# Two graph layers on one core: the back-transform of the convolution cut into small pieces and tied to places in VectorE's queue

## The chip, the cores and the metric

The kernel runs on one core of a Trainium2 chip. The core's engines work from queues of their own: TensorE (PE, with its weight loads shown as PEld), VectorE (DVE), ScalarE (ACT), GpSimd (POOL), and SyncE (SP), which here only starts DMAs. Each engine takes its instructions in the order in which they stand in its queue; semaphores tie the engines together. The time is the device time of one execution in microseconds, and the median of several executions counts.

## The reference, cut to what matters

64 graphs of 256 nodes with 256 features. Layer 0 normalizes the adjacency matrix and multiplies; layer 1 has a convolution of 17 taps along the nodes, a message step with a soft adjacency, and a GRU cell. Each layer ends in a residual and a layer norm. All in float32.

```python
# layer 0
deg = adjacency_matrix.sum(axis=-1)
norm_adj = d_inv_sqrt[:, :, None] * adjacency_matrix * d_inv_sqrt[:, None, :]
h = jnp.einsum('bnm,bmf->bnf', norm_adj + alpha_eff * eye, x)
x = _layernorm(x + jnp.einsum('bnf,pf->bnp', h, W) + b)
# layer 1
h = relu(_bn(_conv1d(xc, conv1_w, 0), ...))
h = _bn(_conv1d(h, conv2_w, 8), ...)              # 17 taps along the nodes
x_conv = transpose(relu(h + xc))
A = jnp.exp(-dist) * mask                          # dist from three columns s of each node
x_nmp = jnp.einsum('bnm,bmd->bnd', A, relu(x @ w_msg.T + b_msg))
gi = concatenate([x_conv, x_nmp]) @ w_ih.T + b_ih
gh = x @ w_hh.T + b_hh
r, z = sigmoid(gi_r + gh_r), sigmoid(gi_z + gh_z)
x = _layernorm(x + (1 - z) * tanh(gi_n + r * gh_n) + z * x)
```

## The kernel before

The 64 graphs go in four groups (NQ = 4) of 16 (Q = 16). The long convolution is done in the frequency domain: the 256 nodes of a graph are cut into 8 tiles of 32 (GT = 8), each transformed over 48 points (FL = 48), so that a group gives 128 rows of every frequency. A group passes through these stages:

1. `layer0` (line 325) and `layer1` (390) for each graph. They are generators: every `yield` ends a piece, and the caller decides what is traced between two pieces. `layer0` has 3 pieces, `layer1` 7. On VectorE `layer0` ends with two scalar_tensor_tensor on x1 (line 383) and a layer norm; `layer1` adds a bias to h, once for each half of the nodes (410), and to msg (431), and multiplies aT by the adjacency (468). The fourth piece of `layer1` makes the forward transform (p_dft, 442), and ACT copies it to V (447).
2. `products` (515): in 12 steps the 23 complex frequencies, and the real ones in step 0, are multiplied by the transformed taps, three real products for a complex one. ACT and DVE write the results to M. V and M are the same tile VM, [128, 48, 256], under two names; so V of the next group can't be written before M of this one has been read.
3. The transform back, in place in M, all on VectorE: `real_transform` and `complex_begin` alongside the products, and `complex_end` (680) after them, made of `four` (560), `four_turned` (645), `turned` (588) and `output` (666). Each `output` writes a pair of points over all tiles to DRAM (xc_d) by a DMA in SP's queue. `complex_end` ends 18 pieces, of four to eight VectorE instructions each.
4. The gates, `gru` (753), for each graph, in 4 pieces: seven products for the first two gates by a scheme that saves an eighth (p_rz, 767), n (p_n, 804), the mixing with x1 and the layer norm. Before it come `load_conv`, `load_gate`, `residual` (a DMA of POOL's queue that adds x1 to the convolution's result), `transposed` and `input_sums` (POOL). All of it needs the convolution's result xc_d of the whole group.

Since V and M share a tile, the next group's first graphs are transformed into a tile of their own, V2, while this group is still being transformed back: AHEAD = 6 of 16 graphs. After `complex_end`, four ACT copies (984) bring V2 into V, and the other ten graphs follow with V as their goal, with four gate graphs (EARLY) in between, two pieces to a graph. The other 12 gate graphs, `late`, lie beside the next group's products, transform back and graphs ahead.

What is traced where is set at lines 949 to 991. In group 0 there are no gates yet: during the steps pieces of `begin` (the next group's graphs ahead) are taken, 2 to 4 per step, and then `merge(begin, end, 3)` traces one piece of `end` after every third of `begin`. In groups 1 and 2, 14 pieces of `late` go with the steps, then come 20 more with 6 of `begin` and 5 of `end`, then the graphs ahead with two pieces of `end` and two or three of `late` at each. In group 3, 14 of `late` go with the steps, and the rest is merged with `end`, two to one; then come all 16 gate graphs of group 3.

The order of tracing isn't that of the queues. A scheduler in the compiler makes the order of each engine's queue beforehand: by its own model of times it takes, among the instructions whose inputs it holds to be ready, the one traced first. So an instruction traced later goes ahead of an earlier one that is not ready yet. The queues are fixed after that; on the chip an instruction that waits holds up all behind it on its engine. Tiles come from pools with a fixed number of buffers: four PSUM banks for the layers (`bank`) and four for products and gates (`accbank`).

Of the kernel before, what the change touches and what calls it, by code (L numbers as in the profile page):

```python
# [14 lines left out]
P = 128  # L15
# [11 lines left out]
def kernel(  # L27
# [55 lines left out]
    def accbank(name):  # L83
        return psacc.tile([P, 512], F32, tag="acc", name=name)

# [239 lines left out]
    def layer0(g):  # L325
# [56 lines left out]
        for c in range(NCH):  # L382
            nc.vector.scalar_tensor_tensor(
                x1[:, c, :], p[:, c, :], dis[:, c : c + 1], x_t[:, c, :], op0=ALU.mult, op1=ALU.add
            )
# [4 lines left out]
    def layer1(g, V, place):  # L390
# [13 lines left out]
        for c in range(NCH):  # L404
            p = bank("p_conv1")[:, : D + NSE]
            for k in range(DCH):
                nc.tensor.matmul(  # L407
                    p, x1T[:, k, c * P : (c + 1) * P], wc1[:, k, :], start=k == 0, stop=k == DCH - 1
                )
            nc.vector.tensor_tensor(h[:, c, :], p, bc1, op=ALU.add)  # L410
# [20 lines left out]
        nc.vector.tensor_tensor(msg, p, bmsg_t.unsqueeze(1).to_broadcast([P, NCH, D]), op=ALU.add)  # L431
# [36 lines left out]
        nc.vector.tensor_mul(aT, aT, adjT[:, :, 0:3:2, :])  # L468
# [91 lines left out]
    def four(re, im):  # L560


        by = im - re
        sub2(blocks(re, by, 2), blocks(re + 2, by, 2))
        sub2(blocks(re, by), blocks(re + 1, by))
        add2(M[:, re + 2, :], M[:, im + 3, :])
        sub2(M[:, im + 2, :], M[:, re + 3, :])
# [31 lines left out]
    def real_transform():  # L599
# [13 lines left out]
        four(8, 12)  # L613
# [31 lines left out]
    def four_turned(re, im, angle):  # L645
# [4 lines left out]
        c2, t2 = turned(re + 2, im + 2, 2 * angle)  # L650
        stt(z[2], t2, -c2, z[0], op0=ALU.mult, op1=ALU.add)
        stt(z[0], t2, c2, z[0], op0=ALU.mult, op1=ALU.add)
        yield
        c1, t1 = turned(re + 1, im + 1, angle)
        c3, t3 = turned(re + 3, im + 3, 3 * angle)
        stt(z[3], t3, -c3 / c1, t1, op0=ALU.mult, op1=ALU.add)
        stt(t1, t3, c3 / c1, t1, op0=ALU.mult, op1=ALU.add)
        stt(z[1], t1, -c1, z[0], op0=ALU.mult, op1=ALU.add)
# [5 lines left out]
        yield  # L664

    def output(q, n, re, im):
# [5 lines left out]
        by = [real_part(t[:, j, :], x, y, 2 * math.pi * (n + 16 * j) / FL) for j in range(2)]  # L672
        low = min(re, im)
# [4 lines left out]
        )  # L678

    def complex_end(q):  # L680

        four(CR, CI)
        yield
        for outs in (((0, 0, 0), (8, 1, 0)), ((4, 2, 0), (12, 3, 1))):
            for n, i, exchanged in outs:
                output(q, n, (CR, CI)[exchanged] + i, (CI, CR)[exchanged] + i)
            yield

        add2(M[:, CR + 4 : CR + 6, :], M[:, CI + 6 : CI + 8, :])
        sub2(M[:, CI + 4 : CI + 6, :], M[:, CR + 6 : CR + 8, :])  # L690
        yield
        for n, re, im, angle in ((2, CR + 4, CI + 4, math.pi / 4), (6, CI + 6, CR + 6, 3 * math.pi / 4)):
            low = min(re, im)
            c, t = turned(re + 1, im + 1, angle)
            stt(blocks(low + 1, 16), t, -c, blocks(low, 16), op0=ALU.mult, op1=ALU.add)
            stt(blocks(low, 16), t, c, blocks(low, 16), op0=ALU.mult, op1=ALU.add)
            yield
            output(q, n, re, im)
            output(q, n + 8, re + 1, im + 1)
            yield  # L700
        for n, re, im, angle in ((1, CR + 8, CI + 8, math.pi / 8), (3, CI + 12, CR + 12, 3 * math.pi / 8)):
            yield from four_turned(re, im, angle)
            output(q, n, re, im)
            output(q, n + 8, re + 1, im + 1)
            yield
            output(q, n + 4, re + 2, im + 2)
            output(q, n + 12, im + 3, re + 3)
            yield
# [44 lines left out]
    def gru(g):  # L753
# [26 lines left out]
        nc.vector.tensor_add(first, half(p15), brz_t)  # L780
# [6 lines left out]
        nc.vector.tensor_add(trz[:, 1:3], trz[:, 1:4:2], half(p34))  # L787
# [7 lines left out]
        for c in range(NCH):  # L795
# [13 lines left out]
            nc.vector.tensor_add(gn, p.rearrange("p (i d) -> p i d", i=2), bn_t)  # L809
# [17 lines left out]
            nc.vector.scalar_tensor_tensor(y, t, 3.0, y, op0=ALU.add, op1=ALU.mult)  # L827
# [31 lines left out]
    def run(stage):  # L859
        for _ in stage:  # L860
            pass

# [59 lines left out]
    gate = ctx.enter_context(tc.tile_pool(name="gate", bufs=2))  # L922
    ahead = ctx.enter_context(tc.tile_pool(name="ahead", bufs=1))


    AHEAD = 6
    V2 = ahead.tile([P, FL, DCH, AHEAD * GT], F32, name="V2")
    EARLY = 4
# [19 lines left out]

    late = nothing()
    for q in range(NQ):  # L950
# [3 lines left out]
        if more:  # L954
            if q:
                others = [both(take(late, 3 if i % 3 == 0 else 2), take(end, 2)) for i in range(AHEAD)]
# [5 lines left out]
        for step in range(STEPS):  # L962
# [5 lines left out]
            if q:  # L968
                run(take(late, (0, 1, 1, 1, 1, 1, 2, 1, 2, 1, 2, 1)[step]))
            else:  # L970
                run(take(begin, 2 + step // 4))
        run(real)
        if not q:
            run(merge(begin, end, 3))
        elif more:
            run(merge(merge(take(late, 20), take(begin, 6), 3), take(end, 5), 5))
            run(begin)
        else:
            run(merge(late, end, 2))
        if more:  # L980
            run(late)
            run(end)
            for f in range(0, FL, 12):
                nc.scalar.copy(V[:, f : f + 12, :, : AHEAD * GT], V2[:, f : f + 12])
            early = gates(q, range(EARLY))
            others = [take(early, 2) for _ in range(Q)]
            run(graphs(first, range(AHEAD, Q), V, others))
            run(early)
            late = gates(q, range(EARLY, Q))
# [55 lines left out]
```

## Time and profile before

| | us |
|---|---|
| runs | 2195.01, 2198.28, 2193.91; median 2195.01 |
| the profiled execution's own time | 2197.18 |
| its span, first to last instruction | 2195.4 |
| mean granted TensorE clock over the span | 0.981 |

The page gives each engine's busy time and its share of the span. Its second part cuts the span into 40 slices of some 55 us; a digit is the busy share in tenths. A stretch of the trace can be asked for by its bounds: the answer has the busy time of each engine in it, the number of instructions in brackets, the granted TensorE clock, and the share and rate of the DMA engines. Matmuls overlap one another, so the time from one to the next is less than the 380 ns that a record of one shows.

The four groups' products begin on PE about 298, 690, 1190 and 1690 us into the span. After about 1960 us only gates of group 3 are left. These rows are the costliest of VectorE's on the tile VM over the whole span (line, operation, count; busy us, mean ns):

| line | what | x | us, ns |
|---|---|---|---|
| 546, 547 | subtract, and 2x - y, of `sub2` | 104 each | 72.6, 698; 72.4, 696 |
| 675 | the two points of `output` | 128 | 55.3, 452 |
| 575, 577 | `real_part` | 100, 72 | 45.4, 465; 30.4, 427 |
| 583, 585 | `imaginary_part` | 24, 20 | 14.5, 605; 9.9, 495 |

In all VectorE is busy 491.65 us with instructions on VM, of 1554.1.

### The profile page before, as it was taken

What the parts mean: (1) busy time and instruction counts of PE and PEld (TensorE: products, weight loads), DVE (VectorE), ACT (ScalarE), POOL (GpSimd) and SP (SyncE); (2) the same over time, 40 slices, a digit from 0 to 9 for tenths busy, and PEclk for the clock granted to TensorE, in tenths of its full rate; (3) what the DMA queues carried; (4) which work ended last, traced back from release to release, by engine and by line L of the source; (5) the groups of instructions that cost most, each with busy time, mean ns of one, the idle gap of its engine ahead of it and who ended that gap; (6) DMA issues with size and microseconds to landing.
All of it is one profiled execution on the core that took longest, in us unless ns stands there. A gap on an engine that the chain in (4) does not pass through costs nothing.

```text
span 2195.4 us, 28939 instructions
## 1 busy us (share of the span) xinstructions
PE 2070.3 (94%) x9805; PEld 1754.5 (80%) x9805; DVE 1554.1 (71%) x3743; ACT 828.8 (38%) x1838; POOL 664.1 (30%) x641
## 2 busy tenths in 40 slices
PE   5999989969999997999999998899999999899998
PEld 4878768758888886888888887788888887678887
DVE  5555548875568799655556889855555879977666
ACT  2656533445441122456552222446553112222222
POOL 2444310113321234223222224322231223344442
PEclk8999989979999999999999999999999999999999
DMA  3766657443337644333335654433333654444441
GB/s 98 222 194 201 218 159 223 154 134 115 99 112 220 201 120 125 115 101 107 108 113 174 204 163 121 130 106 113 103 95 117 207 163 116 119 120 111 104 113 54
DMA packets 251823, 305.83 MB, mean 139 GB/s; under 512 B 18797, under 2 KB 230337, under 8 KB 251674
## 3 DMA queue, kind: packets, MB, share of 16 engines
q1 hardware_dynamic: 183338, 199.93, 30.0%
q10 hardware_dynamic: 45280, 68.04, 8.8%
q0 software_dynamic: 23056, 36.01, 8.3%
q8 instruction: 78, 1.28, 0.2%
q14 instruction: 71, 0.57, 0.1%
HBM read 200.79 MB, written 103.12 MB: 138 GB/s over the span
## 4 chain that ended last, share of the span: by engine, by line
PE 50%; DVE 14%; issue 6%; POOL 6%; ACT 4%; DMA 0%; ACTq 0%; POOLq 0%; SPq 0%; DVEq 0%
PE p_rz L767 18%; PE p_n L804 9%; PE p_k L497 8%; PE p_nmp L473 2%; PE p_out L379 2%; PE p_dft L442 2%; PE p_conv L407 2%; PE p_hT L369 2%; POOL sums L749 1%; POOL ln_rs L304 1%; PE p_msg L428 1%; PE p_dist L466 1%; POOL sums L751 1%; POOL sums L750 1%; DVE gn L809 1%
## 5 line engine op out<-in xcount | busy, mean ns | idle before, releaser
L767 PE MATMUL p_rz<-wrz,sums 128*128 128x256 f32 x1536 | 357.4, 384 | 19.4 <-DVE gn L809 9.8
L804 PE MATMUL p_n<-wn,inputs 128*128 128x256 f32 x1536 | 351.2, 381 | 16.1 <-DVE first L780 15.5
L767 PEld LDWEIGHTS p_rz<-wrz,sums 128*128 128x128 f32 x1536 | 289.8, 191 | 70.9 <-issue 15.8
L804 PEld LDWEIGHTS p_n<-wn,inputs 128*128 128x128 f32 x1536 | 285.8, 190 | 61.8 <-DVE first L780 18.5
L767 PE MATMUL p_rz<-wrz,inputs 128*128 128x256 f32 x1152 | 272.6, 380 | 1.5 <-ACT inputs L739 1.5
L304 POOL TENSOR_TENSOR ln_rs<-ln_rs,neg_half 128x2 f32<-128x2 f32 x129 | 100.3, 777 | 538.9 <-DVE ln_rs L303 453.1
L767 PEld LDWEIGHTS p_rz<-wrz,inputs 128*128 128x128 f32 x1152 | 216.9, 190 | 32.6 <-ACT inputs L739 3.5
L340 POOL TENSOR_TENSOR dis<-deg,neg_half 128x2 f32<-128x2 f32 x64 | 48.5, 758 | 428.8 <-DVE deg L338 322.7
L816 ACT ACTIVATE nn<-gn 128x256 f32<-128x256 f32 x128 | 53.2, 416 | 324.9 <-DVE gn L813 324.5
L497 PE MATMUL p_k<-u,VM 128*128 128x256 f32 x736 | 175.1, 380 | 0.0
L314 ACT ACTIVATE x_g<-x_g,ln_mr,ln_rs 128x256 f32<-128x256 f32 x128 | 70.0, 593 | 256.4 <-DVE ln_mr L312 256.4
L497 PEld LDWEIGHTS p_k<-u,VM 128*128 128x128 f32 x736 | 138.6, 190 | 19.6 <-DMA u<-ud 0.8
L407 PE MATMUL p_conv<-wc,xn 128*128 128x259 f32 x512 | 130.4, 398 | 14.4 <-ACT xn L399 13.8
L442 PE MATMUL p_dft<-fwd,h 128*128 128x240 f32 x512 | 119.8, 378 | 24.3 <-ACT h L411 23.4
L748 POOL TENSOR_TENSOR sums<-inputs 128x384 f32<-128x384 f32 x64 | 69.5, 1086 | 230.4 <-issue 172.2
L369 PE MATMUL p_hT<-adjT,x 128*128 128x256 f32 x512 | 125.9, 391 | 8.3 <-DVE adjT L352 8.1
L442 PEld LDWEIGHTS p_dft<-fwd,h 128*128 128x128 f32 x512 | 97.1, 194 | 40.9 <-ACT h L411 32.9
L473 PE MATMUL p_nmp<-aT,msg 128*128 128x256 f32 x512 | 123.8, 385 | 2.6 <-DVE aT L468 2.6
L407 PEld LDWEIGHTS p_conv<-wc,xn 128*128 128x128 f32 x512 | 98.6, 196 | 34.5 <-ACT xn L399 18.8
L379 PE MATMUL p_out<-w,hT 128*128 128x256 f32 x512 | 124.2, 386 | 0.9 <-ACT hT L374 0.7
L362 POOL TENSOR_TENSOR x_t<-x_t,b_t 128x512 f32<-128x512 f32 x64 | 84.6, 1323 | 128.5 <-ACT x L361 88.3
L428 PE MATMUL p_msg<-wmsg,xn 128*128 128x256 f32 x512 | 122.8, 383 | 0.0
(153 smaller groups left out, 3852.5 us busy)
## 6 DMA issues: line engine op xcount, KB each, us to landing
u<-ud SPq DMA_DIRECT2D x284, 256.0 KB
xn_d<-xn ACTq DMA_DIRECT2D x64, 512.0 KB
inputs<-xn_d SPq DMA_DIRECT2D x64, 512.0 KB
ud<-u_set POOLq DMA_DIRECT2D x39, 480.0 KB, 6.2
adj_t<-in_adj_dram SPq DMA_DIRECT2D x64, 256.0 KB
x_t<-in_x_dram SPq DMA_DIRECT2D x64, 256.0 KB
x_d<-x ACTq DMA_DIRECT2D x64, 256.0 KB
x_g<-x_d SPq DMA_DIRECT2D x64, 256.0 KB
```

The source lines that it names most:

```text
L304: nc.gpsimd.tensor_tensor(rs[:, : len(chunks)], rs[:, : len(chunks)], neg_half[:, : len(chunks)], op=ALU.pow)
L314: nc.scalar.activation(y[:, c, :], y[:, c, :], AF.Identity, bias=mr[:, c : c + 1], scale=rs[:, c : c + 1])
L362: nc.gpsimd.tensor_tensor(x_t, x_t, b0_t.unsqueeze(1).to_broadcast([P, NCH, D]), op=ALU.add)
L369: nc.tensor.matmul(p[:, k, :], x1[:, mc, k * P : (k + 1) * P], adjT[:, mc, 1 - mc : 3 - mc, :].rearrange("p n q -> p (n q)"), start=mc == ...
L379: nc.tensor.matmul(p[:, c, :], hT[:, k, c * P : (c + 1) * P], w0[:, k, :], start=k == 0, stop=k == DCH - 1)
L407: nc.tensor.matmul(p, x1T[:, k, c * P : (c + 1) * P], wc1[:, k, :], start=k == 0, stop=k == DCH - 1)
L428: nc.tensor.matmul(p[:, c, :], x1T[:, k, c * P : (c + 1) * P], wmsg[:, k, :], start=k == 0, stop=k == DCH - 1)
L442: nc.tensor.matmul(p[:, t0 * FL : t1 * FL], h[:, c, k * P : (k + 1) * P], fwd[:, first : first + t1 - t0, :].rearrange("p t f -> p (t f)") ...
L473: nc.tensor.matmul(p[:, k, :], msg[:, mc, k * P : (k + 1) * P], aT[:, mc].rearrange("p n q -> p (n q)"), start=mc == 0, stop=mc == NCH - 1,)
L497: nc.tensor.matmul(p[:, j * D : (j + 1) * D], v[:, k, :], u[:, k, :], start=k == 0, stop=k == DCH - 1)
L767: nc.tensor.matmul(p[:, j * D : (j + 1) * D], a[:, k], wrz[:, b, k], start=k == 0, stop=k == HALF - 1)
L804: nc.tensor.matmul(p[:, o * D : (o + 1) * D], lhsT, w, start=j == 0, stop=j == len(part) - 1)
```

## The change

Four things are changed.

- The pieces of the transform back become small: `four`, `four_turned`, `output` and `complex_end` yield after every two VectorE instructions. `real_transform` still runs its `four` at once.
- Six places in `layer0` and `layer1` and five in `gru` are marked (`mark`): the x1 operations, both h, msg and aT; `first`, the sum trz[:, 1:3], both gn, and y. A new function `paced` runs a main stage and, after each of its pieces, adds a rate for each instruction that was marked in it; for every whole unit it traces one piece of the transform back under `tc.issue_after(i)`. That gives each instruction which the piece traces on VectorE an edge to the marked one, so that the scheduler can't put it ahead of it in VectorE's queue. It is an edge of order alone, with no semaphore. Other engines' instructions, the output DMAs among them, get none.
- In group 0, 12 graphs are made ahead in place of 6, into a V2 of twice the size. For room, the pool `gate` is opened only once this V2 is closed, after the copies to V; four graphs remain to be made beside the four early gate graphs, with five pieces of `early` at each in place of two. From group 1 on V2 has 6 graphs as before.
- What is traced beside what: `end` no longer goes with the graphs ahead by `both`, nor by `merge`, but by `paced` with the rates 1.2, 0.85, 0.85 and 1.15 pieces for each mark in the four groups. In group 0 each step takes 3 pieces of `begin`. In group 3 a step takes `step % 2` pieces of `late`, 6 in all.

```diff
+    def paced(main, other, rate):
+
+        marks.clear()
+        due = 0
+        for _ in main:
+            for i in marks:
+                due += rate
+                while due >= 1:
+                    due -= 1
+                    with tc.issue_after(i):
+                        next(other, "end")
+            marks.clear()
+            yield
...
-            nc.vector.tensor_tensor(h[:, c, :], p, bc1, op=ALU.add)
+            mark(nc.vector.tensor_tensor(h[:, c, :], p, bc1, op=ALU.add))
...
-        nc.vector.tensor_add(first, half(p15), brz_t)
+        mark(nc.vector.tensor_add(first, half(p15), brz_t))
...
         sub2(blocks(re, by, 2), blocks(re + 2, by, 2))
+        yield
         sub2(blocks(re, by), blocks(re + 1, by))
+        yield
         add2(M[:, re + 2, :], M[:, im + 3, :])
+        yield
         sub2(M[:, im + 2, :], M[:, re + 3, :])
...
         by = [real_part(t[:, j, :], x, y, 2 * math.pi * (n + 16 * j) / FL) for j in range(2)]
+        yield
         low = min(re, im)
...
-    gate = ctx.enter_context(tc.tile_pool(name="gate", bufs=2))
-    ahead = ctx.enter_context(tc.tile_pool(name="ahead", bufs=1))
-
-
-    AHEAD = 6
-    V2 = ahead.tile([P, FL, DCH, AHEAD * GT], F32, name="V2")
     EARLY = 4
+
+    def open_ahead(graphs):
+
+        scope = ExitStack()
+        pool = scope.enter_context(tc.tile_pool(name="ahead", bufs=1))
+        return scope, graphs, pool.tile([P, FL, DCH, graphs * GT], F32, name="V2")
...
+    RATES = (1.2, 0.85, 0.85, 1.15)
+
+
+    scope, AHEAD, V2 = open_ahead(12)
     late = nothing()
     for q in range(NQ):
...
-                others = [both(take(late, 3 if i % 3 == 0 else 2), take(end, 2)) for i in range(AHEAD)]
+                others = [take(late, 3 if i % 3 == 0 else 2) for i in range(AHEAD)]
...
-                run(take(late, (0, 1, 1, 1, 1, 1, 2, 1, 2, 1, 2, 1)[step]))
+                run(take(late, (0, 1, 1, 1, 1, 1, 2, 1, 2, 1, 2, 1)[step] if more else step % 2))
             else:
-                run(take(begin, 2 + step // 4))
+                run(take(begin, 3))
         run(real)
         if not q:
-            run(merge(begin, end, 3))
+            run(paced(begin, end, RATES[q]))
         elif more:
-            run(merge(merge(take(late, 20), take(begin, 6), 3), take(end, 5), 5))
-            run(begin)
+            run(paced(chain(merge(take(late, 20), take(begin, 6), 3), begin), end, RATES[q]))
         else:
-            run(merge(late, end, 2))
+            run(paced(late, end, RATES[q]))
+            run(end)
         if more:
             run(late)
             run(end)
             for f in range(0, FL, 12):
                 nc.scalar.copy(V[:, f : f + 12, :, : AHEAD * GT], V2[:, f : f + 12])
+            if q == 0:
+                scope.close()
+                gate = ctx.enter_context(tc.tile_pool(name="gate", bufs=2))
             early = gates(q, range(EARLY))
-            others = [take(early, 2) for _ in range(Q)]
+            others = [take(early, 5 if q == 0 else 2) for _ in range(Q)]
             run(graphs(first, range(AHEAD, Q), V, others))
             run(early)
+            if q == 0:
+                scope, AHEAD, V2 = open_ahead(6)
+                ctx.enter_context(scope)
             late = gates(q, range(EARLY, Q))
```

## The prediction

> **What bounds the kernel now.** I read the page's busy shares and its 40 slices first, then the windows around the dips, the waits of PE there, the timeline inside the deepest dip, and the chain of waits last.
>
> ```profile
> PE 2070.3 (94%) x9805; PEld 1754.5 (80%) x9805; DVE 1554.1 (71%) x3743; ACT 828.8 (38%) x1838; POOL 664.1 (30%) x641
> ...
> PE   5999989969999997999999998899999999899998
> ...
> DVE  5555548875568799655556889855555879977666
> ...
> PEclk8999989979999999999999999999999999999999
> ```
>
> PE is busy 94%, but its slices dip four times (slices 9, 16, 25, 35), each time where DVE shows 8 or 9. Each dip follows the products of one group of 16 graphs, where DVE transforms back. The windows on those stretches (length, PE busy, PE weight loads, DVE, ACT, POOL, granted clock, DMA share, GB/s):
>
> ```profile
> 414.00:478.00 64.00, 43.85 (x202) 34.13 (x200) 61.88 (x177) 26.25 (x61) 8.54 (x8) 0.90 0.40 128
> 478.00:500.00 22.00, 20.39 (x79) 15.96 (x80) 9.47 (x31) 14.84 (x31) 10.81 (x11) 0.75 0.64 155
> 780.00:920.00 140.00, 125.51 (x576) 105.20 (x575) 127.04 (x302) 46.88 (x103) 52.54 (x46) 0.96 0.46 129
> 1290.00:1410.00 120.00, 105.22 (x478) 88.51 (x477) 117.55 (x269) 33.76 (x73) 43.48 (x38) 0.96 0.44 123
> 1800.00:1960.00 160.00, 141.85 (x649) 118.41 (x648) 150.48 (x307) 35.59 (x72) 62.24 (x55) 1.00 0.41 114
> ```
>
> The same windows for VectorE's instructions on the transform's tile VM alone:
>
> ```profile
> 414.00:478.00 64.00, 46.41 (x111) 0.90 0.40 128
> ...
> 1290.00:1410.00 120.00, 56.40 (x113) 0.96 0.44 123
> 1800.00:1960.00 160.00, 67.34 (x124) 1.00 0.41 114
> ```
>
> And the stretch ahead of the last dip, where group 3's products run:
>
> ```profile
> 1690.00:1800.00 110.00, 110.00 (x517) 96.67 (x516) 87.98 (x170) 20.29 (x40) 21.45 (x19) 1.00 0.69 208
> ```
>
> I price lost PE time as stretch minus matmuls times full-rate pitch. That pitch is 110/517 = 0.213 us in the last line, 188.20/916 = 0.2055 in the layer-rich stretch from 500 to 690, about 0.2105 for mixtures. Lost: 414 to 500: 86 - 281 x 0.2055 = 28 us. 780 to 920: 140 - 576 x 0.2105 = 19. 1290 to 1410: 120 - 478 x 0.2105 = 19. 1800 to 1960: 160 - 649 x 0.211 = 23. Together 89 us of 131 lost in all (2195.4 - 9805 x 0.2105); most of the rest is setup and tail, which the change leaves alone.
>
> Why PE loses is plainest in the first dip (timeline: start, duration, instruction, idle time before it in brackets):
>
> ```profile
> 461.54 17.36 SPq L676 DMA_DIRECT2D xc_d<-VM  x8
> ...
> 468.33 0.43 DVE L410 TENSOR_TENSOR h<-p_conv,bc 128x259 f32<-128x259 f32 x1
> ...
> 469.73 0.63 ACT L411 ACTIVATE h<-h 128x512 f32<-128x512 f32 x1 [9.30 <-DVE h L410]
> ...
> 470.41 3.56 PE L442 MATMUL p_dft<-fwd,h 128*128 128x240 f32 x8 [9.56 <-ACT h L411]
> ```
>
> From 458.7 to 468.3 DVE does transform operations back to back (L662, L577, L675 and so on); the h addition, whose matmuls were done at 458.7, waits behind them, then ACT, then PE for 9.56 us. The scheduler held the transform operations to be ready sooner. In the three later dips no single wait is so long: DVE is 90 to 98% full and PE loses 0.5 to 3.9 us at a time, for `first` (L780), gn (L809) and xn.
>
> **What the Trainium skill says.** "TensorE: Matmul & The Clock Gate", section "What's actually happening", says that an idle window of about 3.4 us throttles the PE clock until a busy window releases it. The trace agrees: after the 9.56 us wait the clock is 0.75 (second window), while the last dip, made of short waits, stays at 1.00. So closing long gaps pays twice. "Perfetto Trace Analysis", section "Optimization Strategy", says that where the contended engine changes over time, interleaving the regimes may help; the trace has such regimes: DVE 97% in the first dip, 61% (115.95 of 190) from 500 to 690. "SBUF — State Buffer", section "SBUF: two separate sides", says that DVE operations with two SBUF inputs and GpSimd lock each other out of a shared port; the trace's 256-element transform operations take 386, 416 and 1215 ns (least, median, most), in line with it. So a transform operation costs more among gates, where POOL is busier: 46.41/111 = 0.42 us beside layers, 56.40/113 = 0.50 and 67.34/124 = 0.54 beside gates. No page prices an order edge.
>
> **The change, part by part.** *The back-transform's work* is the same: 116 DVE instructions per group (32 pairs for 16 outputs, 8 in `four`, 44 others) and 16 output DMAs on SP. Cut at the new yields it has 4 + 8 + 2 + 12 + 32 = 58 pieces of two instructions, 0.84 us each beside layers, 1.0 to 1.1 beside gates.
>
> *The edge* adds no wait: a piece only stands behind the marked operation on DVE's queue. It forbids the block seen at 458 to 468. Behind each mark one or two pieces (0.8 to 2 us) may delay what follows on DVE: trz behind `first`, L810 behind gn, the second h; PE waits for the first two through banks. I cost this at nothing where DVE has idle time, since the next operation of a chain is usually not ready at once; it is the bad rival below. POOL, ACT and SP get no edge; SP's output DMAs follow data, one at a time instead of eight together (17.36 us), so the loads behind them go earlier.
>
> *Group 0.* The steps take 3 pieces of `begin` each, 36 as before (2 to 4). Of 12 graphs ahead, 9 remain: 90 main pieces, 9 x 6 = 54 marks; at 1.2 all 58 pieces are out by mark 48.3, graph 8 of 9. A layer graph costs PE 13.2 us (about 64 matmuls x 0.2055) and DVE 7.4 (rows of section 5 and of the groups by line, 7.2; from 500 to 690 115.95 less 4.6 gate graphs at 10.5, over 9.1 layer graphs, 7.4). Pieces add 7.2 x 0.84 = 6.0: DVE 13.4 against PE 13.2. So it is just saturated for 8 graphs: 2 us short, and 6 for waits at a full queue (estimate: PE's small waits in the later dips are 1 to 2 us per 15). Left 8 to 9 of 28: gain 19. Against it: V2 is twice as large, so the four ACT copies (12 x 1159 ns for three groups) take about 9.3 us rather than 4.6, and the gate pool opens only after them. Graph 12's PE work and two layer0 cover this, not wholly: 2 us back. Net 17. Then 4 graphs instead of 10 stand beside 4 gate graphs; each graph's 13.2 us hides the first loads. The remaining five `early` pieces per graph sum to the same 20.
>
> *Groups 1 and 2.* The products are unchanged. Then 34 gate pieces (8.5 gate graphs at 5 marks) and 8 graphs of layer work give about 82 marks; at 0.85 the end is out by mark 68. A gate graph costs PE 70 x 0.211 = 14.8, DVE 8.7 packed ((219.73 - 126.28)/10.7 from 1690 to 1936) to 10.5 (1960 to 2100: 99.29 over 9.45). Pieces add 5 x 0.85 x 1.0 = 4.2: 12.9 to 14.7 against 14.8. Before, the first five gate graphs carried about 7 us of transform each. So DVE is full but no longer over. I leave 8 of 19 us: gain 11 each, 22. The end is out long before the V copies.
>
> *Group 3.* The steps now take 6 gate pieces rather than 14, so 42 (10.5 graphs, 53 marks) run under the end; at 1.15 its last piece stands behind mark 51. Per graph 8.7 + 5 x 1.15 x 1.09 = 15.0 on DVE against 14.8: saturated, not over. Steps: PE 60 (284 x 0.211) + 1.5 x 14.8 = 82; DVE 59 + 13 to 16, fits. Last transform operation at 1690 + 84 + 155 = 1929 (1934.4 now). Behind it the chain to group 3's first sums: xc write (2.9 us, 1934.47 to 1937.37), xc load (3.2 to the accumulating DMA at 1940.54), that DMA, about 3, transposes, ACT, POOL sums (0.6 + 0.9 + 1.1): about 13. The work left for PE then is about 4 us, so some 9 are bare, where before gates covered most. The sums' matmuls start at 1943 to 1949 instead of 1953.8. Gain 6.
>
> Sum 17 + 22 + 6 = 45: from the profiled execution's own 2197.2 us (span 2195.4) to 2152. The median of the runs, 2195.0, is 2.2 lower; forecast 2150.
>
> **The rivals.**
> A. As above: own range 2132 to 2170. Chance 0.48.
> B. Everything recovered: 79 of the 89 us, 2116. For it: total DVE work is below PE's in every group. Against: DVE full at the rates of groups 0 and 3. 0.10.
> C. Only the long block goes: group 0 gains 17, the gate stretches stay DVE-bound, since 10.5 + 4.2 already meets 14.8 and waits come on top: 2178, 2164 to 2197. 0.21.
> D. Slower: the pins sit at the gates' bank releases. `first` (L780) and gn (L809) are among five marks, and PE already waits 15.5 us in 12 waits for one and 9.8 in 9 for the other. If a piece of 0.84 us lands between each and the next release, each of the 27.5 gate graphs loses 1.7 us more and nothing of the gate stretches is won: +46 - 17 = +29, 2224. It decides from 17/27.5 = 0.6 us per gate graph beyond today's loss. For it: a full in-order DVE queue; against: fewer pieces per gate graph than now in groups 1 and 2. Group 3's bare chain, up to 13 us, adds to it. 0.21.
>
> **How the numbers follow.** About 0.2% (4.4 us) is what a measurement here tells from no change. Faster: A, B and most of C (0.16): 0.74. Same: 0.03 of C and 0.03 of D: 0.06. Slower: 0.02 of C, 0.18 of D: 0.20. The range from 2126 to 2206 holds A, C, about two fifths of D and a third of B; some 0.19 is outside.
>
> **What would show it.** Right: no DVE block of transform operations over 3 us beside layers; no PE wait over 4 us and a clock at 1.00 from 415 to 540; PE at 94% or more in the three later stretches; 12 x 1.16 us copies become 8 of 1.16 and 4 of 2.3. Wrong: waits for `first` and gn growing beyond 50 us in sum (D); DVE at 97% with PE below 90% in the gate stretches (C); a PE gap over 13 us ahead of group 3's gates, or PE starved in its steps.

## The result, and the profile after

The changed kernel takes 2190.7 us (median of four runs, 2189.66 to 2191.19) against 2195.4 for the kernel before beside it (four runs): 0.9976 of its time, interval 0.9959 to 0.9994. The forecast was 2150. The sign was right and the size was not: some 5 us came where 45 were forecast. The profiled execution has a span of 2188.8 us against 2195.4.

The page's busy shares and its slices after:

```profile
PE 2071.8 (95%) x9805; PEld 1753.1 (80%) x9805; DVE 1558.0 (71%) x3743; ACT 831.9 (38%) x1838; POOL 654.3 (30%) x641
...
PE   5999999988999998999999999899999999989998
...
DVE  5555558786568798865557889875556989967766
...
PEclk8999999999999999999999999999999999989999
```

The dip to 6 in slice 9 is gone from PE's row; the clock's dip that stood there is gone too, and another stands in slice 36. Shallow dips to 8 remain at slices 9 and 10, 16, 26 and 36. The same four stretches as before, the first 6 us earlier, the third 10 (columns as in the prediction):

```profile
408.00:494.00 86.00, 75.41 (x363) 59.16 (x362) 70.00 (x212) 48.71 (x114) 18.84 (x20) 1.00 0.38 124
780.00:920.00 140.00, 130.04 (x607) 109.54 (x606) 121.63 (x283) 51.05 (x111) 47.10 (x46) 0.98 0.42 120
1280.00:1400.00 120.00, 111.29 (x527) 95.45 (x526) 108.73 (x235) 38.62 (x84) 44.08 (x43) 0.99 0.43 119
1800.00:1960.00 160.00, 141.63 (x631) 119.87 (x630) 133.37 (x279) 35.21 (x73) 60.25 (x58) 0.94 0.42 114
```

Counted as the prediction counted them, the stretches lose 11 us (86 - 363 x 0.2055; 28 before), 12 (19), 9 (19) and 27 (23). A reader who stopped here would book 17 + 7 + 10 - 4 = 30 us of gain. The span is only 6.6 us shorter, and most of that comes from elsewhere. So the stretches must be completed to whole stages. A stage runs here from the start of a group's first matmul into p_real to the next group's. In the kernel before these starts are at 297.7, 652.4, 1171.8 and 1689.7 us; the 690 and 1190 given ahead of the prediction for the second and third group are too late. So the stretch from 500 to 690, which gave the pitch of 0.2055, holds 38 us of group 1's products; 500 to 652 alone has 739 matmuls in 152 us, 0.2057 for each, and the pitch stands. In the table, "ahead" is from the first p_dft (group 0's own graphs) to group 0's products, and the last stage runs to the end of the span:

| us | ahead | group 0 | group 1 | group 2 | group 3 | span |
|---|---|---|---|---|---|---|
| before | 248.1 | 354.6 | 519.5 | 517.9 | 505.7 | 2195.4 |
| after | 241.7 | 355.1 | 515.5 | 513.0 | 513.5 | 2188.8 |
| difference | -6.4 | +0.5 | -4.0 | -4.9 | +7.8 | -6.6 |
| forecast | 0 | -17 | -11 | -11 | -6 | |

Group 0 gives all its gain back inside its own stage, groups 1 and 2 keep 4 and 5 us of 7 and 10, group 3 loses, and 6 us come from a place that the prediction didn't look at.

**Ahead.** POOL around 275 us in the kernel before (timeline: start, duration, instruction, idle time before it in brackets):

```profile
274.57 0.99 POOL L748 TENSOR_TENSOR sums<-inputs 128x384 f32<-128x384 f32 x1 [11.11 <-DMA x_g<-x_d]
275.52 0.71 POOL L340 TENSOR_TENSOR dis<-deg,neg_half 128x2 f32<-128x2 f32 x1
276.19 0.71 POOL L304 TENSOR_TENSOR ln_rs<-ln_rs,neg_half 128x2 f32<-128x2 f32 x1
```

One of the sums for gate graph 0, which PE first reads at 410 us, had been put ahead of dis and ln_rs of the layers. It waits 11.11 us for its DMA, and the layers wait behind it: between 240 and 300 us PE waits 5.3 us for h at one place (wait, us in all, times, longest):

```profile
PE p_dft L442 <- ACT h L411: 5.3, 1, 5.3
```

After, the gate pool opens only after the copies to V, so nothing of the gates can stand there.

**Group 0's handover.** Three more windows after, and the timeline at the copies:

```profile
494.00:520.00 26.00, 23.86 (x115) 18.64 (x114) 20.63 (x65) 15.09 (x36) 5.52 (x5) 1.00 0.32 102
520.00:560.00 40.00, 32.28 (x150) 26.23 (x149) 14.25 (x51) 26.62 (x48) 12.55 (x14) 0.91 0.60 178
560.00:647.00 87.00, 84.75 (x403) 71.50 (x404) 53.17 (x113) 30.88 (x70) 31.95 (x31) 1.00 0.32 88
```

```profile
529.77 4.13 ACT L1016 COPY VM<-V 128x2304 f32<-128x2304 f32 x2
...
536.33 2.11 ACT L1016 COPY VM<-V 128x2304 f32<-128x2304 f32 x1 [0.50 <-ACT xn L485]
...
538.35 0.58 ACT L407 COPY xn<-p_x1T 128x512 f32<-128x512 f32 x1
538.98 3.82 PE L415 MATMUL p_conv<-wc,xn 128*128 128x259 f32 x8 [5.61 <-ACT xn L407]
```

From 520 to 560 PE does 150 matmuls: 40 - 150 x 0.2055 = 9 us are lost, at a clock of 0.91. ACT is in V2's four copies, of 2.1 us each, and what PE needs from ACT (xn) stands behind them: PE waits 5.61 us. Another 2 us go from 494 to 520 and 4 after 560. The kernel before at its own handover and behind it:

```profile
500.00:560.00 60.00, 59.83 (x297) 50.38 (x296) 33.29 (x91) 31.69 (x76) 16.44 (x18) 1.00 0.31 93
560.00:652.00 92.00, 90.37 (x444) 76.32 (x443) 54.81 (x140) 44.69 (x104) 28.93 (x29) 1.00 0.35 101
```

Over the whole stage the kernel before lost 2 + 28 - 1 + 1 = 30 us (554, 281, 297 and 444 matmuls in windows from 298, 414, 500 and 560 to 652), the changed one 3 (548 matmuls from 292 to 408) + 11 + 2 + 9 + 4, about 30 again.

**Group 1's handover.** The window and the timeline where its gate graphs end and the next layers begin, after:

```profile
836.00:862.00 26.00, 20.01 (x84) 16.35 (x83) 24.70 (x50) 7.80 (x18) 12.71 (x12) 0.87 0.54 150
862.00:960.00 98.00, 93.27 (x451) 77.24 (x450) 78.23 (x212) 45.55 (x103) 24.22 (x23) 1.00 0.35 113
```

```profile
835.68 1.03 PE L385 MATMUL p_out<-w,hT 128*128 128x256 f32 x4
...
839.86 2.24 DVE L596 SCALAR_TENSOR_TENSOR turn<-VM 128x256 f32<-128x256 f32 x1
...
844.18 0.86 DVE L390 SCALAR_TENSOR_TENSOR x<-p_out,dis,x_t 128x256 f32<-128x256 f32 x2
...
855.76 3.82 PE L415 MATMUL p_conv<-wc,xn 128*128 128x259 f32 x8 [3.17 <-ACT xn L407]
```

26 - 84 x 0.2105 = 8 us are lost in these 26: p_out is done at 836.7, but x1's addition starts at 844.18, behind a queue of transform pieces and gate work on DVE (24.70 busy of 26.00). PE has gate products to do until 852.6, with waits of 1.27 us for POOL's sums and 1.55 for `first`; then only the new graph's chain is left, and it waits 3.17 for xn. The clock in the window is 0.87. Another 5 us go from 862 to 960.

**Group 3's end.** After, at the last output:

```profile
1932.13 0.51 SPq L692 DMA_DIRECT2D xc_d<-VM  x1
...
1934.81 9.96 SPq L729 DMA_DIRECT2D xc_g<-xc_d  x3
...
1938.85 1.24 POOL L740 DMA_DIRECT2D xc_g<-x_d  x1 [12.14 <-DMA xc_g<-xc_d]
...
1943.27 1.11 PE L751 MATMUL p_xcT<-ident,xc_g 128*128 128x128 f32 x4 [9.97 <-DMA xc_g<-x_d]
...
1947.61 5.44 PE L781 MATMUL p_rz<-wrz,sums 128*128 128x256 f32 x18
```

The gates of group 2 are used up; PE waits 9.97 us for output, load and addition, before the transposes can start. Measured from the start of its own products the last output is at 1932.1 - 1675.3 = 256.8 us, where it was at 244.7 before: it comes 12 us later, with nothing left beside it.

PE's waits over the whole span, after:

```profile
PE p_conv L415 <- ACT xn L407: 23.2, 18, 5.6
PE p_n L818 <- DVE first L794: 13.0, 11, 3.0
PE p_dft L450 <- ACT h L419: 12.2, 18, 2.4
PE p_xcT L751 <- DMA xc_g<-x_d: 10.8, 2, 10.0
```

### The profile page after: what moved, and what is told of

Same layout as the page of the kernel before. It is cut to its first block, busy times and chain, and to the rows that moved or that the text cites. A ratio compares the mean times of both kernels' runs of the same rounds, so it can differ in the third digit from the quotient of the medians.

```text
span 2188.8 us, 28989 instructions
## 1 busy us (share of the span) xinstructions
PE 2071.8 (95%) x9805; PEld 1753.1 (80%) x9805; DVE 1558.0 (71%) x3743; ACT 831.9 (38%) x1838; POOL 654.3 (30%) x641
## 4 chain that ended last, share of the span: by engine, by line
PE 42%; DVE 11%; issue 7%; POOL 5%; ACT 4%; DMA 1%; ACTq 0%; POOLq 0%; SPq 0%; DVEq 0%
PE p_rz L781 16%; PE p_n L818 8%; PE p_k L505 7%; PE p_nmp L481 2%; PE p_hT L375 2%; POOL ln_rs L310 1%; PE p_out L385 1%; PE p_dft L450 1%; POOL sums L764 1%; POOL sums L765 1%; POOL sums L763 1%; PE p_conv L415 1%; PE p_msg L436 1%; PE p_dist L474 1%; ACT inputs L753 1%
## 5 line engine op out<-in xcount | busy, mean ns | idle before, releaser
L781 PE MATMUL p_rz<-wrz,sums 128*128 128x256 f32 x1536 | 352.5, 382 | 5.1 <-POOL sums L764 2.6
```

The costliest lines, as they stand in the source:

```text
L781: nc.tensor.matmul(p[:, j * D : (j + 1) * D], a[:, k], wrz[:, b, k], start=k == 0, stop=k == HALF - 1)
```

## The experiments

Theory: the transform pieces cost what was forecast; the gain is given back at three handovers (V2's copies in group 0, gates to layers in 1 and 2, the end of group 3). Rivals: the edges themselves cost it; the pieces still cost PE as much as before; 12 graphs ahead are the wrong place. Each was timed beside the kernel before. Stages, in us, of one profiled execution each (the ratio is that of the times). That execution can lie off the median of its runs, by some 3 us at most in ten of the rows; e1's lies 4.3 below it, e11's 6.4 above:

| | ahead | g0 | g1 | g2 | g3 | span | median | ratio, interval |
|---|---|---|---|---|---|---|---|---|
| e1_gate_late | 240.3 | 360.5 | 519.6 | 518.2 | 505.7 | 2190.5 | 2196.6 | 0.9999, 0.999 to 1.0008 |
| e2_last_old | 240.0 | 355.8 | 515.4 | 512.9 | 505.8 | 2177.2 | 2181.3 | 0.9935, 0.9921 to 0.995 |
| e3_copies_dve | 240.2 | 348.6 | 515.8 | 512.7 | 514.0 | 2178.3 | 2183.2 | 0.9947, 0.9933 to 0.9961 |
| e4_no_edges | 240.2 | 356.5 | 519.7 | 518.6 | 507.5 | 2189.6 | 2193.2 | 0.9989, 0.9981 to 0.9996 |
| e5_both | 241.6 | 348.4 | 518.4 | 512.7 | 505.6 | 2177.3 | 2176.2 | 0.992, 0.9908 to 0.9933 |
| e6_no_back0 | 241.6 | 340.7 | 515.6 | 513.7 | 505.6 | 2167.9 | 2169.6 | 0.9887, 0.9874 to 0.9901 |
| e7_pace_last | 239.9 | 349.4 | 517.6 | 512.7 | 507.0 | 2173.0 | 2175.1 | 0.9919, 0.9906 to 0.9932 |
| e8_first_old | 240.1 | 365.3 | 514.3 | 512.7 | 505.7 | 2184.4 | 2187.0 | 0.9972, 0.9963 to 0.9981 |
| e9_two_rates | 239.7 | 349.3 | 512.7 | 510.2 | 505.6 | 2163.9 | 2166.3 | 0.9882, 0.9867 to 0.9897 |
| e10_no_back1 | 240.0 | 349.3 | 500.4 | 514.9 | 505.7 | 2157.5 | 2159.2 | 0.9849, 0.9835 to 0.9862 |
| e11_nine | 241.5 | 362.2 | 514.2 | 515.1 | 506.3 | 2189.7 | 2185.0 | 0.9969, 0.9957 to 0.998 |
| e12_three_tenths | 241.5 | 348.2 | 519.6 | 517.0 | 505.8 | 2183.2 | 2182.2 | 0.9941, 0.9927 to 0.9954 |

Group 1, with nothing changed in it, takes 514.2 to 518.4 in e2, e3, e5 to e8 and e11: something of what is changed elsewhere moves it a little. A difference of under some 4 us in one stage is not read as an effect below, unless two groups or the timed ratio show it too.

**e1_gate_late.** The kernel before with the gate pool opened after the copies, V2 at 6 graphs.

```diff
+            if q == 0:
+                scope.close()
+                gate = ctx.enter_context(tc.tile_pool(name="gate", bufs=2))
```

> The kernel before with one part of the change alone: V2 keeps 6 graphs, but the pool gate opens only after the copies of V2 to V in group 0. Theory: of the 6.6 us that the changed kernel gained, about 6 were won before the first product, where POOL no longer stands 11 us at a sum of gate graph 0 that had been put far ahead; so this alone gives about 2189, ratio 0.997. Rival: that stall went because of 12 graphs ahead or 3 pieces per step; then this gives 2195, ratio 1.000.

The 8 us ahead of the products came (248.1 to 240.3): the sum no longer stands there, and PE's wait of 5.3 us for h is 0.2. But group 0 became 5.9 longer, and the time is that of before: the rival's number, but not its reason. The place was right, the net was wrong. Where the 5.9 go was not isolated; PE's one long wait in that group is 11.2 us for h, where it was 9.6. The gain ahead of the products is in the changed kernel too; whether the loss is, with twelve graphs ahead, no run shows.

**e2_last_old.** The change, with group 3 in the order of before: 14 pieces of late in the steps, the rest two to one with coarse pieces of the end, no edges.

```diff
-                run(take(late, (0, 1, 1, 1, 1, 1, 2, 1, 2, 1, 2, 1)[step] if more else step % 2))
+                run(take(late, (0, 1, 1, 1, 1, 1, 2, 1, 2, 1, 2, 1)[step]))
...
-            run(paced(late, end, RATES[q]))
+            run(merge(late, coarse(end), 2))
```

> The changed kernel with group 3 as before: 14 gate pieces in its steps, then two gate pieces to one of the 18 old pieces of the transform back, without edges. Theory: group 3 lost about 8 us by the change, through the bare chain from the last output to the transposes (10 us of PE waiting, then a clock of 0.74); so this is faster than the changed kernel, about 2183, ratio 0.9945 to before. Rival: the chain only takes the place of losses that return when the group is DVE-bound again: 2190, ratio 0.9976.

As the theory has it: group 3 is back at 505.8, and no other stage moves by more than 1.5 us. The last output comes 244.8 us after the start of the products instead of 256.8. Group 3's end in the changed kernel, and the like window here:

```profile
1930.00:1960.00 30.00, 19.20 (x79) 15.98 (x78) 13.00 (x27) 5.15 (x11) 12.73 (x12) 0.77 0.49 114
```

```profile
1911.00:1941.00 30.00, 27.01 (x122) 21.80 (x121) 24.25 (x48) 8.44 (x17) 15.62 (x14) 1.00 0.51 143
```

PE does 122 matmuls instead of 79, at a clock of 1.00 instead of 0.77.

**e3_copies_dve.** The change, with V2's four copies of group 0 on VectorE, which has room there (busy 14.25 of 40 us).

```diff
-                nc.scalar.copy(V[:, f : f + 12, :, : AHEAD * GT], V2[:, f : f + 12])
+                (nc.scalar.copy if q else nc.vector.tensor_copy)(
+                    V[:, f : f + 12, :, : AHEAD * GT], V2[:, f : f + 12]
+                )
```

> The changed kernel with the four copies of V2 to V in group 0 on VectorE in place of ScalarE. Theory: PE waited 5.6 us for xn behind the copies (2.1 us each) on ScalarE and then ran at a clock of 0.90; VectorE is 60 to 70% idle there; gain about 6, 2184. Rival: the layers' chain runs through VectorE as well and waits there as long: 2190, within 2 us of the changed kernel.

Group 0 takes 348.6: the copies on ACT cost 6.5 us more than on VectorE, where they are also shorter, 1.35 us each; what each of the two is worth was not separated. The handover's window:

```profile
516.00:556.00 40.00, 36.59 (x180) 29.75 (x179) 21.18 (x59) 20.27 (x48) 16.99 (x18) 1.00 0.62 183
```

180 matmuls instead of 150 in 40 us, ACT 20 instead of 27 busy, and the clock at 1.00.

**e4_no_edges.** The change without the order edges, everything else kept.

```diff
-                    with tc.issue_after(i):
-                        next(other, "end")
+                    next(other, "end")
```

> The changed kernel without the edges: the same small pieces traced at the same places, free to be put ahead in VectorE's queue. Theory (the edges hinder the block and are worth having): blocks of transform operations return, PE waits of 5 us and more in group 0, 5 to 15 us slower than the changed kernel, 2196 to 2206. Rival (the edges hold back the layers' and gates' chains, by the marks at their heads): faster than the changed kernel, 2175 to 2187.

Neither was met: 0.9989 lies between. Without edges groups 1 and 2 take 519.7 and 518.6, which is before's time, so the edges are worth 4 to 6 us in each; in group 3 they cost 6 (507.5 without). That rests on the stages: the intervals of the two ratios, 0.9989 here and 0.9976 with edges, overlap. Without them the scheduler puts the end out early (219 us after the start of the products in group 3; 241 in groups 1 and 2, as in the kernel before). The edges are a gain where their delay is covered, a loss where it isn't.

**e5_both.** e2 and e3 together.

> The changed kernel with both mends: the four copies of V2 in group 0 on VectorE, and group 3 in the old order. Theory: the two costs lie 1100 us apart and add up: 14.3 us below before for the one, 6.4 more for the other, 2174, ratio 0.9906. Rival: part of each is noise of the start; then no better than 2180, ratio 0.9935.

0.992 (interval to 0.9908) where the two gains would add up to 0.9906: they add up nearly, in their stages exactly (348.4 and 505.6); what is missing is 3 us in group 1, within the spread of that group. This is the base of what follows.

**e6_no_back0.** e5, with group 0's transform back left out but for its output DMAs: 116 VectorE instructions less, so the convolution's result of that group is not computed.

```diff
-        end = complex_end(q)
+        end = complex_end(q) if q else only_outputs(q)
```

> As the kernel with both mends, but the 116 VectorE instructions of the transform back after the products are left out in group 0; its 16 output DMAs stay, spread over the same stage. Theory: the pieces still cost PE, by small waits: a layer graph takes 14.3 us with them (424 to 510 in the changed kernel) and 13.0 without (263 to 276), so 9 graphs give about 12 us: ratio 0.985, 2162. Rival: at 80% VectorE hides them, and the layers' own chain sets the 14.3 us: within 3 us of the kernel with both mends.

Group 0 takes 340.7, 7.7 less than e5: between the two. So the pieces cost about 7.7 us there, near what the prediction had left (8 to 9). They take their outputs with them: with nothing to wait for, the 16 output DMAs go out 61 to 114 us after the start of the products, where e5's last is at 231. But 340.7 is only 14 below before, where the prediction had counted 28 as lost. In this order of twelve graphs ahead PE loses time without any transform:

```profile
408.00:494.00 86.00, 80.64 (x394) 65.25 (x394) 42.34 (x133) 51.78 (x123) 17.52 (x20) 1.00 0.32 104
494.00:520.00 26.00, 24.26 (x120) 19.79 (x119) 13.65 (x42) 15.97 (x38) 5.29 (x6) 1.00 0.31 101
```

86 - 394 x 0.2055 = 5 us and 1 us, with DVE half idle: layer graphs alone don't fill PE. Its largest wait from 412 to 517 is for xn, 5.8 us in 8 waits of at most 0.7. With gates in the mix, from 500 to 652 before, nothing is lost (60 + 92 - (297 + 444) x 0.2055 = 0).

**e7_pace_last.** e3, with group 3's 14 pieces in the steps, but the end still paced by edges, at 1.7 in place of 1.15.

```diff
-    RATES = (1.2, 0.85, 0.85, 1.15)
+    RATES = (1.2, 0.85, 0.85, 1.7)
```

> The changed kernel with the copies on VectorE, and in group 3 14 gate pieces in the steps as before but the paced end at 1.7 pieces for a mark, so that its last piece stands behind mark 34 of 43. Theory: what hurt group 3 is when the end is out, not the edges; 9 marks (some 26 us of gates) cover the chain to the next gates: as the kernel with both mends or up to 4 us better, ratio 0.989 to 0.991. Rival: at 8.5 pieces to a gate graph VectorE is over its time and the edges cost: 5 us or more worse than both mends, ratio 0.993 or more.

Group 3 takes 507.0 and the end is out after 247.1 us: with edges it is nearly as short as without, and the ratio is that of e5, as the theory has it. So the cause is when the end is out, not the edge.

**e8_first_old.** e5, with group 0 in the order of before (6 graphs ahead, coarse merge, no edges, early pieces of two), the gate pool still late and the copies on VectorE.

```diff
-    scope, AHEAD, V2 = open_ahead(12)
+    scope, AHEAD, V2 = open_ahead(6)
...
-            run(paced(begin, end, RATES[q]))
+            run(merge(begin, coarse(end), 3))
```

> As the kernel with both mends, but group 0 in the old order: 6 graphs ahead, 2 to 4 pieces of them per step, the old 18 pieces of the transform back merged one to three without edges; the copies on VectorE and the late gate pool stay. Theory: twelve graphs ahead with pacing and six with the block cost PE about the same in group 0 (45 us of loss each), so within 4 us of both mends, 2172 to 2180. Rival: with the handover mended, twelve ahead are worth 8 us or more: 2183 and up.

The rival holds: group 0 takes 365.3, 17 more than e5, and the times differ by 11 us. But the copies on VectorE do not suit the old order: e1, the same order and pool with the copies on ACT, takes 360.5. Against that e5 gains 12 in group 0; against the kernel before, whose pool was open from the start (354.6), it gains 6.

**e9_two_rates.** e5, with two rates in groups 1 and 2: 0.5 pieces for each mark beside the gates, 0.95 after.

```diff
-            run(paced(chain(merge(take(late, 20), take(begin, 6), 3), begin), end, RATES[q]))
+            run(paced(merge(take(late, 20), take(begin, 6), 3), end, 0.5))
+            run(paced(begin, end, 0.95))
```

> As the kernel with both mends, but in groups 1 and 2 the pieces go at 0.5 to a mark beside the five gate graphs and at 0.95 after them, in place of 0.85 throughout. Theory: the 6 us gap of PE at the handover from gates to layers (840 to 860 in the changed kernel) is VectorE's backlog, at 94% busy with gates and pieces, with the x1 operations 7.5 us late in its queue; with 15 pieces in place of 25 there it goes: 4 to 8 us in each group, ratio 0.985 to 0.988. Rival: the gap belongs to the handover itself (load, layer norm, xn), or the loss moves to the layers: within 2 us, ratio 0.991 to 0.993.

Between the two, close to the theory: 512.7 and 510.2, below all other readings of these groups with the transform in them, and by the ratios 8 us below e5 (0.38%), where 4 to 8 in each group were expected. This is the fastest complete version here: 0.9882, 26 us below the kernel before by that ratio. Its windows about group 1's handover:

```profile
752.00:827.00 75.00, 75.00 (x361) 66.03 (x361) 66.06 (x133) 21.72 (x47) 31.06 (x30) 1.00 0.48 123
827.00:853.00 26.00, 22.66 (x105) 18.91 (x104) 22.08 (x52) 11.36 (x26) 8.74 (x9) 0.93 0.33 83
853.00:962.00 109.00, 101.85 (x487) 85.29 (x486) 89.08 (x241) 48.55 (x107) 27.67 (x27) 0.98 0.36 117
```

26 - 105 x 0.2105 = 4 us are lost at the handover instead of 8; the layers behind lose 9 (109 - 487 x 0.2055) instead of 5, and the gates ahead nothing.

**e10_no_back1.** e5, with group 1's transform back left out but for its output DMAs, as e6 did for group 0.

```diff
-        end = complex_end(q)
+        end = only_outputs(q) if q == 1 else complex_end(q)
```

> As the kernel with both mends, but the 116 VectorE instructions after the products are left out in group 1, the 16 output DMAs stay. Theory: group 1 took 519.4 us before and 515.5 changed, for all that 19 us were counted as lost; without the pieces it takes 505 or less, so that the pieces still cost PE over 10 us: ratio 0.987. Rival: most of what was counted as lost belongs to the gates and layers themselves: 511 to 514, ratio 0.990 to 0.991.

As the theory has it: group 1 takes 500.4, 19 below before, just what the prediction had counted as lost, and 15 below after (by the ratios 16 below e5). Here the floor is real, and the pieces still cost 15 where the prediction left 8. As in e6 the outputs go early too, the last 121 us after the start of the products (314 in e5). Without the pieces the handover is smooth:

```profile
830.00:850.00 20.00, 19.61 (x98) 16.33 (x97) 12.52 (x27) 10.69 (x25) 9.01 (x9) 1.00 0.29 80
850.00:950.00 100.00, 98.53 (x485) 84.04 (x484) 58.92 (x161) 47.78 (x106) 27.61 (x28) 1.00 0.36 108
```

98 matmuls in 20 us and 485 in 100: nothing lost in either (0.204 and 0.206 us for each).

**e11_nine.** e5 with nine graphs ahead in group 0, rate 1.75, three early pieces to a graph.

```diff
-    scope, AHEAD, V2 = open_ahead(12)
+    scope, AHEAD, V2 = open_ahead(9)
-    RATES = (1.2, 0.85, 0.85, 1.15)
+    RATES = (1.75, 0.85, 0.85, 1.15)
```

> As the kernel with both mends, but 9 graphs ahead in group 0, 1.75 pieces to a mark, three early pieces to a graph. Theory: a layer graph alone on PE takes 13.6 us, with gates 12.2, so three graphs moved back win 4 us, and pieces at 10.5 to a graph instead of 7.2 put VectorE over its time and lose more: 3 to 10 us slower than both mends, ratio 0.9935 to 0.997. Rival: the fewer graphs alone on PE, the better: 2 to 5 us faster, ratio 0.990.

Slower, as the theory has it: by the ratios 11 us. Group 0 takes 362.2, 14 more than e5, in the longest of its six executions. PE's largest waits from 400 to 654 are for adjT from VectorE, 11.4 us in 6. Fewer graphs ahead means more transform to each graph, and PE loses more than layers alone cost it.

**e12_three_tenths.** e9 with 0.3 in place of 0.5.

> As the kernel with two rates, but 0.3 in place of 0.5 beside the gates: 8 pieces there, 50 behind the 53 marks after, so that the last stands at the very end of the graphs ahead. Theory: what is won beside the gates (under 2 us a group, PE has 3.5 us idle left at the handover) is lost where the copies of V2 wait for the end: within 3 us of two rates, ratio 0.9870 to 0.9895. Rival: the fewer pieces beside gates, the better: ratio 0.986 or less.

Both missed it: groups 1 and 2 became 7 longer each than in e9. In group 1 the end is now out 333.9 us after the start of the products instead of 325.2. PE and ACT at V2's copies in that group:

```profile
984.18 3.82 PE L415 MATMUL p_conv<-wc,xn 128*128 128x259 f32 x8 [6.64 <-ACT xn L407]
```

```profile
979.40 1.15 ACT L1024 COPY VM<-V 128x1152 f32<-128x1152 f32 x1 [3.45 <-DMA xc_d<-VM]
...
983.55 0.57 ACT L407 COPY xn<-p_x1T 128x512 f32<-128x512 f32 x1
```

The third of the four copies waits for an output DMA, the fourth and xn stand behind it, and PE waits 6.64 us. So the pace has an optimum between: too many pieces beside the gates and the handover to the layers loses, too few and the end is late at the copies.

## Why the prediction was half right

Where PE loses time and to whom was read rightly, and the sign came out; the size failed. The 45 us were a sum of gains inside four stretches, and what happened at the handovers behind them was put at 2 us in group 0, at nothing in groups 1 and 2; in group 3 the end was forecast 18 us too early. By its own steps:

- *What bounds the kernel* held: PE waits behind DVE where the transform stands. The long block at 458 to 468 is gone, from 408 to 560 no block of transform operations lasts over 2.5 us, and the clock from 408 to 494 is 1.00. "I price lost PE time as stretch minus matmuls times full-rate pitch" held as a count of lost time; in group 1 e10 got all of it back.
- *"Left 8 to 9 of 28: gain 19"* held inside the stretch: 17 came, and over the stage the pieces still cost 7.7 (e6). What failed is to take the 28 as what group 0 can win. With twelve graphs ahead a stage without any transform is only 14 below before (e6): 5 to 6 us are what layer graphs alone lose, now twelve of them rather than six; the rest lies in the handovers, in e6 about 3 us each from 520 and from 560 on. What the transform cost in the old order no run measured.
- *"Graph 12's PE work and two layer0 cover this, not wholly: 2 us back"* is the second term that failed: the copies cost 6.5 (e3). They were sized well (2.3 us forecast, 2.1 measured); what was missed is that ACT stands in PE's own chain, through xn, so that PE waited 5.61 us and then ran at a lower clock. "Net 17" became nothing: 17 gained in the first stretch, then given back, 2 us from 494 to 520, 9 at the handover and 4 after it, where the kernel before lost nothing.
- *"I leave 8 of 19 us: gain 11 each"* failed in size: 15 are left (e10), 4 to 5 are gained. The per-graph sum (DVE 12.9 to 14.7 against PE 14.8) held beside the gates: the 79 us ahead of 836 lose nothing. It was no sum for the change from gates to layers, where DVE still had its backlog and PE soon a single chain: 8 of the 15 are lost there. e9 supports it by moving pieces away: its loss there is 4 instead of 8, and the two groups together take 1022.9 us, 4 below the best of the others (e8, 1027.0) and 8 below e5.
- *"Last transform operation at 1690 + 84 + 155 = 1929"* failed: from its products' start the last output is at 257, not 239. The steps took 83 us (84 forecast), the end behind them 174 in place of 155, with DVE busy 161.42 of them and some 14 lost to PE (754 matmuls at 0.211 make 159), and the gates of group 2 were used up by then. "So some 9 are bare" had the right size (9.97 and 0.83); the clock of 0.77 from 1930 to 1960 came on top. "Gain 6" became a loss of 7.8, which e2 and e7 take back by having the end out at 245 to 247.
- *Ahead of the products* the prediction charged nothing. There the late gate pool removed a stall of POOL worth 6 to 8 us (e1), a side effect of the change. The other four stages sum to -0.6 us, so that even the right sign of the whole came from a place where nothing was forecast: luck.
- *The edge, "I cost this at nothing where DVE has idle time"*: the edges cost less than nothing, and rival D fell. Its sign was waits for `first` and gn over 50 us; they went down, from 15.5 and 9.8 to 13.0 and 0.6. e4 shows that the edges gain about 10 us in groups 1 and 2 and give 6 back in group 3.
- *The signs*: the one on PE at 94% in the later stretches failed everywhere (130.04/140 = 93%, 93%, 89%), and "no PE wait over 4 us from 415 to 540" failed at the very end of its range, at 538.98. Rival C, "only the long block goes" with 2178, is the nearest to what came and its range holds it, but for another reason than its own: group 0 did not keep its 17, the gate stretches in groups 1 and 2 did get better, and the end of group 3 was lost.

"TensorE: Matmul & The Clock Gate" in the Trainium skill, section "What's actually happening", explains why these waits cost more than their length: an idle stretch of about 3.4 us throttles the clock. The runs agree on the long waits: 5.61 us of wait with 0.91 in its window of 40 us, 9.97 us with 0.77 in one of 30; where e3 and e2 close the wait, the like windows read 1.00. But the clock is 0.87 at group 1's handover too, where the longest single wait is 3.17 us: in these runs 3.4 is no sharp limit, and waits a little shorter were not free.

Three things stay open. The 5 us that layers beside pieces still lose from 862 to 960 (9 in e9) were located, but not attributed to a single wait. What group 0 loses by the late gate pool was measured for the old order alone. The spread of 4 us of an unchanged group 1 was seen, not explained.

## What to carry to other kernels

Sum a forecast over whole stages, from one fixed landmark to the next, and not over the stretch that hurts: what is gained there has to survive each handover behind it. At a handover only one chain is left for the bounding engine, so ask what stands in each queue that this chain passes (here ACT's copies and DVE's backlog), not whether the engine has idle time on average. Spreading work evenly delays its end: check from the stage's start when the last piece is out, and what is left to cover the chain behind it.

## What the runs showed of the hardware, beyond what was expected

- A gate's sum, put far ahead in POOL's queue, stopped POOL for 11.11 us on a DMA with two short operations of the layers behind it; where it could no longer stand there (e1), the stage was 8 us shorter.
- A 256-element scalar_tensor_tensor on the transform's tile, 0.42 us as a rule beside layers, took 2.24 us at 839.86. "SBUF — State Buffer" in the Trainium skill, section "SBUF: two separate sides", says that a DVE operation with two SBUF inputs and a GpSimd operation that reads SBUF lock each other out. The trace after agrees: all 363 such operations during which no POOL instruction ran took 0.38 to 0.43 us, and of the 109 that met one, 19 took over 0.7, the longest 2.58. No run here took POOL away.
- A copy of 128 x 2304 float32 from V2 to V took 2.11 to 2.13 us on ACT (after) and 1.33 to 1.36 on DVE (e3).
- Before the first forward transform 46.3 to 51.0 us pass in these runs, in whose setup nothing differs: single spans a few microseconds apart are compared by stages or by timed ratios, not by themselves.
